# The opening of a cross-attention and feed-forward kernel: loads, second block's normalisation and values in another order

## The chip, the cores and the metric

The kernel runs on one core of a Trainium2 chip. The metric is the device time of one execution in microseconds (us), lower is better. A core has TensorE (PE, with its weight loads shown as PEld), VectorE (DVE), ScalarE (ACT), GpSimd (POOL) and SyncE (SP). SP, ScalarE and GpSimd issue DMA loads, each on a queue of its own. Every engine takes its instructions in the order in which they stand in its program.

## The reference

The input `x` has 2048 tokens of 256 features; the context has 1601 rows of 192 features. The reference normalises the tokens, adds cross-attention over the context, normalises again and adds a feed-forward layer with weights of +1 and -1. Cut to what the change touches:

```python
# 16 heads of 64; a learned null key and null value stand ahead of the 1601 context rows
x = layer_norm(layernorm(x), g_norm)
q = x @ Wq
k, v = split(context @ Wkv)
k, v = concat(null_k, k), concat(null_v, v)          # 1602 keys
sim = einsum(q, k) * scale
sim = where(mask, sim, -big)                         # the null key is always kept
out = layer_norm((softmax(sim) @ v) @ Wout, g_out)
x = x + out
x = x + ffn(layernorm(x))                            # three layers, relu between
```

## The kernel before

The work is cut into 32 units: 8 pairs of heads by 4 blocks of 512 tokens. A unit computes the scores of its block against 13 tiles of 128 keys (`exps`, L372), takes their exponential on ScalarE (L385), sums these on GpSimd (L570, L572, into `acc`), and multiplies them with the values (`weighted`, L392). The shift of each exponential is the exact maximum of the row. It is found beforehand in a cheaper number format: `max_chunk` (L335) multiplies 128 queries of both heads with 512 keys into a buffer of TensorE's accumulation memory (PSUM) and VectorE reduces it (L338). There are 12 such chunks for a block, three key chunks (`CHUNKS`) by four groups of queries, and a thirteenth (`REST`, L319 and L322) for the last 66 keys. Inside a unit the maxima of the next unit are made beside the exponentials of this one.

The first unit has no unit before it, so its keys, queries, values and maxima are made in an opening, and that is what the change is about. The order in the opening is written out by hand, under `tc.manual_schedule()`, and each engine keeps it. Its steps:

- `load_pair(0)` issues on SP the keys' and values' weights (`wa`, `wb`), with the tokens of block 0 (`load_x(0)`) between them and the query and output weights (`wq`, `wo`). The other three blocks follow on SP; the context's four chunks are issued by ScalarE; the mask (`keep`), the norm's gain (`gn_sb`), the null key and value and small things are loaded by GpSimd.
- `input_root` takes the statistics of a block on VectorE (`stats`, L75 and L76) and their root on ScalarE (L422). `input_normed` centres and scales it, on VectorE for block 0 (L87) and on ScalarE, `beside`, for the others (L141, L142). `input_turned` transposes it on TensorE (L437) into `xnT`; `project_q` makes the queries (L200), copied twice by ScalarE (L201, L202).
- `first_keys(n)` makes the keys of one chunk (L211, L212); VectorE masks them (L214) and puts the null key where a key is dropped (L215, with `drop`, the mask reversed, which GpSimd makes at L486).
- `first_values(n)` makes the values of four tiles (L259, L260), and ScalarE copies them (L262).
- `keys_stepped` turns the keys into differences on GpSimd (L248), which `exps` needs.
- `max_combined` joins the maxima (L343), `max_turned` transposes them (L348) and VectorE spreads them into `shifts` (L350).

PSUM buffers come from two pools of two: `flex` and `spare`. `slot` takes them in turn, and a buffer is free again when the engine that reads it is done.

Eight semaphores serve the loads of SP and ScalarE in turn, so a load waits on its queue until the load eight before it has landed.

In the opening before, the two key chunks, the queries and the first eight maxima come first. Then VectorE takes the statistics of block 1, and the last four chunks of maxima follow with values 0 and 1 between them, then the transposes of block 1, the rest chunk, value group 2, the queries of block 1 and value group 3:

```python
        xn = input_root(1)
        input_normed(1, *xn, beside=True)
        ...
        for t in range(4):
            max_chunk(0, 0, 3 * t + 2, slot)
            if t % 2 == 1:
                first_values(t // 2, slot)
        input_turned(1, slot)
        max_chunk(0, 0, REST, slot)
        first_values(2, slot)
        max_combined(0, 0)
        project_q(0, 1, slot)
        max_turned(0, 0)
        first_values(3, flex)
```

Of the kernel before, what the change touches and what calls it, by code (L numbers as in the profile page):

```python
# [9 lines left out]
F32 = mybir.dt.float32  # L10
F32R = mybir.dt.float32r
U8 = mybir.dt.uint8
AF = mybir.ActivationFunctionType
ALU = mybir.AluOpType
# [6 lines left out]
KEYS = M + 1  # L21
CD = 192
HEADS, DH = 16, 64
# [3 lines left out]
NB = N // 512  # L27
# [3 lines left out]
REST = 12  # L31
# [5 lines left out]
def xattn_ffn(ctx, tc, x, ctxT, mask, g_norm, null_kv, wq, wkv, wout, g_out, k0, k1, k2, s0, s1, s2, out):  # L37
# [29 lines left out]
    ones = cp.tile([128, DH], F32, name="ones")  # L67
    warm = cp.tile([128, 1], F32, name="warm")

    def stats(src, n, name):  # L70

        mv = sp.tile([128, 4, 2], F32, tag="mv", name=f"mv_{name}")
        for j in range(n):
            st = sp.tile([128, 6], F32, tag="st", name=f"st_{name}_{j}")
            nc.vector.bn_stats(st, src[:, j, :])  # L75
            nc.vector.bn_aggr(mv[:, j, :], st)  # L76
        return mv

    def rstd_of(mv, n, name, scale=1.0, bias=None):
# [64 lines left out]
    with ExitStack() as att:  # L144
# [21 lines left out]
        def load_pair(p):  # L166
            wq_t = pp.tile([128, 2, 128], F32, tag="wq", name=f"wq_{p}")
            wa_t = pp.tile([128, 2, 128], F32, tag="wa", name=f"wa_{p}")
            wb_t = pp.tile([128, 2, 128], F32, tag="wb", name=f"wb_{p}")
            wo_t = lp.tile([128, D], F32, tag="wo", name=f"wo_{p}")  # L170
            both = wkv.rearrange("r (k w) -> r k w", k=2)[:, :, ts(p, 128)]
            nc.sync.dma_start(out=wa_t, in_=both[0:128])
            nc.sync.dma_start(out=wb_t[:64], in_=both[128:CD])
            if p == 0:

                nc.gpsimd.memset(wb_t[64:], 0.0)
                load_x(0)
            else:
                nc.sync.dma_start(out=wb_t[64:], in_=both[128:CD])
            nc.sync.dma_start(out=wq_t, in_=wq[:, ts(p, 128)].rearrange("(c r) w -> r c w", c=2))  # L180
            nc.sync.dma_start(out=wo_t, in_=wout[ts(p, 128), :])
            weights[p] = (wq_t, wa_t, wb_t, wo_t)


# [65 lines left out]
        def first_values(n, get):  # L250

            v = pairs[0][1]
            tiles = range(4 * n, min(4 * n + 4, KC))
            rows = 128 if n < 3 else KLAST
            ps = get(f"psv_0_{n}")
            for i, t in enumerate(tiles):
                keys = ds(128 * t, rows)
                out_t = ps[:rows, 0, ts(i, 128)]
                nc.tensor.matmul(out_t, ctx_a[:, keys], weights[0][1][:, 1, :], start=True, stop=False)  # L259
                nc.tensor.matmul(out_t, ctx_b[:, keys], weights[0][2][:, 1, :], start=False, stop=True)  # L260
            w = len(tiles)
            nc.scalar.copy(  # L262
                v[:rows, ds(4 * n, w), :], ps[:rows, 0, : 128 * w].rearrange("p (t d) -> p t d", d=128)
            )
            if n == 0:
                nc.vector.tensor_copy(v[0:1, 0, :], nullv)

        def project_v(p, m):

# [146 lines left out]

        def input_root(b):
            mv = stats(x_sb[:, ts(b, 4), :], 4, f"x{b}")  # L420
            r = sp.tile([128, 4], F32, tag="rstd", name=f"rstd_x{b}")
            nc.scalar.activation(r, mv[:, :, 1], AF.Sqrt, bias=eps2_sb, scale=1.0 + EPS)  # L422
            return mv, r

        def input_normed(b, mv, r, beside=False):
            nc.vector.reciprocal(r, r)
            if beside:
                centred_beside(y_sb, x_sb, mv, r, b)
                return
            for j in range(4):  # L430
                centred(y_sb[:, 4 * b + j, :], x_sb[:, 4 * b + j, :], mv, r, j)
# [18 lines left out]
        def load_x(b):  # L450
            nc.sync.dma_start(out=x_sb[:, ts(b, 4), :], in_=x[ts(b, 512), :].rearrange("(c p) d -> p c d", p=128))

        load_pair(0)
        for b in range(1, NB):
            load_x(b)
        for n, (at, w) in enumerate(CHUNKS):
            skip = 1 if n == 0 else 0
            nc.scalar.dma_start(
                out=ctx_a[:, ds(at + skip, w - skip)], in_=ctxT[0:128, ds(at + skip - 1, w - skip)]
            )  # L460
            nc.scalar.dma_start(
                out=ctx_b[:64, ds(at + skip, w - skip)], in_=ctxT[128:CD, ds(at + skip - 1, w - skip)]
            )
        nc.gpsimd.memset(eps2_sb, EPS * EPS)
        nc.gpsimd.memset(eps_sb, EPS)
        make_identity(nc, ident)
        nc.gpsimd.memset(keep[:, 0:1], 0)
        nc.gpsimd.memset(ctx_a[:, 0:1], 0.0)
        nc.gpsimd.memset(ctx_b[:64, 0:1], 0.0)
        nc.gpsimd.memset(ctx_b[64:], 0.0)  # L470
        nc.gpsimd.dma_start(out=keep[:, 1:], in_=mask.partition_broadcast(128))
        nc.gpsimd.dma_start(out=gn_sb, in_=g_norm.rearrange("(c p) -> p c", p=128))
        for j in range(2):
            nc.gpsimd.dma_start(out=nullk[ts(j, DH), :], in_=null_kv[0].rearrange("(p o) -> p o", o=1))
        nc.gpsimd.memset(mcol_u8[0:1, 0:1], 1)
        nc.gpsimd.dma_start(out=mcol_u8[1:128, 0:1], in_=mask[0:127].rearrange("(p o) -> p o", o=1))
        nc.gpsimd.dma_start(
# [4 lines left out]
        )  # L482
        for j in range(2):
            nc.gpsimd.dma_start(out=nullv[:, ts(j, DH)], in_=null_kv[1:2, :])

        nc.gpsimd.tensor_scalar(drop, keep, -1.0, 1.0, ALU.mult, ALU.add)  # L486
        nc.gpsimd.dma_start(out=gout_sb, in_=g_out.partition_broadcast(128))
        for j, s in enumerate((s0, s1, s2)):
            nc.gpsimd.dma_start(out=s_sb[:, j : j + 1], in_=s.partition_broadcast(128))
        nc.gpsimd.memset(mcol, 0.0)  # L490
        nc.gpsimd.memset(maskb, 0.0)
        nc.gpsimd.memset(ones, 1.0)

        nc.scalar.activation(warm, eps_sb, AF.Sqrt)

        open_pair(0)
        xn = input_root(0)
        nc.vector.tensor_scalar(ones_r, ident, 0.0, 1.0, ALU.mult, ALU.add)
        nc.vector.tensor_tensor(pick[:, :, 0], ident[:, 0:4], ident[:, DH : DH + 4], ALU.add)
        input_normed(0, *xn)  # L500
        first_keys(0, slot)
        input_turned(0, slot)
        first_keys(1, slot)
        project_q(0, 0, slot)
        for t in range(4):
            max_chunk(0, 0, 3 * t, slot)
            if t == 1:
                first_keys(2, slot)
        for t in range(4):
            max_chunk(0, 0, 3 * t + 1, slot)  # L510
            if t == 1:
                first_keys(3, slot)
                keys_stepped(0)
        xn = input_root(1)
        input_normed(1, *xn, beside=True)

        nc.scalar.activation(warm, eps_sb, AF.Exp)

        nc.vector.tensor_scalar(maskb[:, : KC - 1], mcol_u8[:, : KC - 1], -MASKED, MASKED, ALU.mult, ALU.add)
        nc.vector.tensor_scalar(  # L520
# [1 line left out]
        )  # L522
        for t in range(4):
            max_chunk(0, 0, 3 * t + 2, slot)
            if t % 2 == 1:
                first_values(t // 2, slot)
        input_turned(1, slot)
        max_chunk(0, 0, REST, slot)
        first_values(2, slot)
        max_combined(0, 0)  # L530
        project_q(0, 1, slot)
        max_turned(0, 0)
        first_values(3, flex)
        begin.__exit__(None, None, None)
        last = None
        with tc.manual_schedule():
# [235 lines left out]
```

## Time and profile before

| what | value |
|---|---|
| median of three runs | 1332.05 us (1331.78 to 1335.83) |
| the profiled execution's own time | 1330.09 us |
| its span, first to last instruction | 1328.3 us |
| mean granted TensorE clock | 0.992 |
| TensorE busy | 1299.5 us (98%) |
| GpSimd busy | 1003.4 us (76%) |
| VectorE busy | 819.9 us (62%) |
| ScalarE busy | 618.9 us (47%) |
| TensorE busy in the first 50 us | 34.06 us |
| VectorE busy in the first 50 us | 27.86 us |
| VectorE waits for the first tokens until | 9.33 us |
| first reduction of maxima begins | 20.95 us |
| first exponential begins | 49.89 us |

The times in the profile are counted from the first instruction of the span. "L338" is line 338 of the kernel before. Busy shares over the whole span are means over the opening, 32 units and the feed-forward part; the opening has its own limits and is read from stretches of its own. A matmul in plain 32-bit numbers is listed as two instructions.

### The profile page before, as it was taken

The numbers are of one execution on the slowest core, as the hardware profiler recorded it, in microseconds if no ns is written. First come the engines' busy times: TensorE is split into PE (matmuls) and PEld (weight loads), VectorE is DVE, ScalarE is ACT, GpSimd is POOL, SyncE is SP. The second block draws the span as 40 slices with busy tenths as digits, with TensorE's granted clock in tenths as the row PEclk, the third lists the DMA queues.
The fourth block names the chain that finished last, engine by engine and source line by source line (L and its number), as shares of the span: only waits on it lengthen the run. The fifth ranks groups of instructions, "written<-read, shape, count | busy, mean of one in ns | idle before, by whom it ended". The sixth has DMA issues, their size and how long they took to land.

```text
span 1328.3 us, 16173 instructions
## 1 busy us (share of the span) xinstructions
PE 1299.5 (98%) x6528; PEld 655.3 (49%) x6528; DVE 819.9 (62%) x817; ACT 618.9 (47%) x676; POOL 1003.4 (76%) x508
## 2 busy tenths in 40 slices
PE   6989999999999999999999999999999999999998
PEld 2534444444444444444444444444444443688887
DVE  6677566666666666666666666667656784554431
ACT  1746444444454455555555555555544556421220
POOL 4478988898888988898889888888898999711100
PEclk9989999999999999999999999999999999999999
DMA  5000000000000000000000000000000010000000
GB/s 140 21 1 4 0 1 13 5 1 0 13 4 2 1 1 12 4 1 1 13 4 1 1 13 4 0 1 5 0 17 1 0 41 1 1 8 8 17 16 17
DMA packets 16091, 13.18 MB, mean 10 GB/s; under 512 B 2624, under 2 KB 15488, under 8 KB 16016
## 3 DMA queue, kind: packets, MB, share of 16 engines
q1 hardware_dynamic: 14640, 10.57, 2.8%
q10 hardware_dynamic: 896, 1.23, 0.3%
q8 instruction: 51, 0.84, 0.3%
q0 software_dynamic: 480, 0.34, 0.1%
q14 instruction: 24, 0.20, 0.0%
HBM read 10.04 MB, written 2.10 MB: 9 GB/s over the span
## 4 chain that ended last, share of the span: by engine, by line
PE 92%; DVE 4%; ACT 2%; DMA 1%; issue 1%; POOL 0%; ACTq 0%; DVEq 0%
PE sT L372 29%; PE av L392 26%; PE ps L668 10%; PE max L335 6%; PE psq L200 4%; PE po L400 4%; PE ps L691 2%; PE den L410 2%; DVE mx L338 2%; PE psv L277 2%; PE psk L225 1%; PE sT L383 1%; PE psv L289 1%; PE psk L230 1%; PE max L319 1%
## 5 line engine op out<-in xcount | busy, mean ns | idle before, releaser
L572 POOL TENSOR_TENSOR acc<-acc,e 128x1024 f32<-128x1024 f32 (+1 forms) x352 | 847.9, 2409 | 27.6
L338 DVE TENSOR_REDUCE mx<-max 128x2 f32<-128x1024 f32 x384 | 455.0, 1222 | 89.2 <-PE max L335 83.5
L385 ACT ACTIVATE e<-sT,maskb 128x1024 f32<-128x1024 f32 (+1 forms) x416 | 460.1, 1114 | 53.9 <-PE sT L383 16.8
L372 PE MATMUL sT<-qT,kT 64*128 64x512 f32 (+1 forms) x1664 | 451.1, 613 | 1.2 <-ACT e L385 1.2
L392 PE MATMUL av<-e,v 128*64 128x512 f32 (+1 forms) x1664 | 369.5, 594 | 0.2 <-ACT e L385 0.2
L335 PE MATMUL max<-kr,qr 64*128 64x512 f32 x768 | 293.3, 752 | 3.1 <-DVE mx L338 2.4
L392 PEld LDWEIGHTS av<-e,v 128*64 128x64 f32 (+1 forms) x1664 | 116.7, 137 | 237.8 <-issue 219.3
L372 PEld LDWEIGHTS sT<-qT,kT 64*128 64x128 f32 (+1 forms) x1664 | 130.2, 181 | 164.3 <-ACT e L385 155.3
L620 ACT COPY avs<-av 128x512 f32<-128x512 f32 x32 | 18.7, 586 | 323.0 <-PE av L392 323.0
L412 DVE RECIPROCAL aoT<-den 128x512 f32<-128x512 f32 x31 | 104.1, 3357 | 60.0 <-PE den L410 60.0
L570 POOL TENSOR_TENSOR acc<-e,e 128x1024 f32<-128x1024 f32 x32 | 76.8, 2399 | 80.3 <-ACT e L385 80.3
L335 PEld LDWEIGHTS max<-kr,qr 64*128 64x128 f32 x768 | 76.6, 188 | 94.0 <-DVE mx L338 46.9
L350 DVE TENSOR_TENSOR mT<-mt,pick 128x512 fp32r<-128x512 f32 x32 | 22.1, 691 | 122.1 <-PE mt L348 122.0
L668 PE MATMUL ps<-h0hi,w 128*128 128x512 f32 x256 | 79.5, 392 | 0.0
L668 PE MATMUL ps<-h0lo,w 128*128 128x512 f32 x256 | 78.9, 389 | 0.0
L120 POOL TENSOR_TENSOR y_sb<-y_sb,gout_sb 128x256 f32<-128x256 f32 x12 | 9.3, 777 | 88.8 <-DVE y_sb L87 88.8
L201 ACT ACTIVATE qr<-psq 128x512 fp32r<-128x512 f32 x32 | 19.1, 597 | 100.4 <-PE psq L200 100.4
L200 PE MATMUL psq<-xnT,wq 128*128 128x512 f32 x128 | 62.0, 608 | 2.5 <-DVE xnT L442 2.5
L657 DVE SCALAR_TENSOR_TENSOR h1lo<-ps,h1hi 128x1024 fp32r<-128x1024 f32 x16 | 19.6, 1224 | 68.3 <-ACT h1hi L656 68.2
L400 PE MATMUL po<-wo,aoT 128*128 128x256 f32 x256 | 60.5, 379 | 0.0
L656 ACT ACTIVATE h1hi<-ps 128x1024 fp32r<-128x1024 f32 x16 | 16.4, 1026 | 94.6 <-PE ps L668 94.6
L248 POOL TENSOR_TENSOR kT<-kT 128x256 f32<-128x256 f32 (+1 forms) x48 | 31.8, 661 | 35.5 <-DVE kr L237 18.8
(150 smaller groups left out, 1067.9 us busy)
## 6 DMA issues: line engine op xcount, KB each, us to landing
x_sb<-in_x SPq DMA_DIRECT2D x4, 512.0 KB, 8.6
out_x<-o SPq DMA_DIRECT2D x8, 256.0 KB, 2.1
wa<-in_wkv SPq DMA_DIRECT2D x8, 128.0 KB, 2.7
wq<-in_wq SPq DMA_DIRECT2D x8, 128.0 KB, 2.2
wo<-in_wout SPq DMA_DIRECT2D x8, 128.0 KB, 2.1
xnT<-in_k SPq DMA_DIRECT2D x1, 1024.0 KB, 5.9
wb<-in_wkv SPq DMA_DIRECT2D x15, 64.0 KB, 2.4
ctx_a<-in_ctxT ACTq DMA_DIRECT2D x2, 256.0 KB, 7.1
```

The lines of the kernel that those rows point to most:

```text
L200: nc.tensor.matmul(ps[:, 0, :], weights[p][0][:, c, :], xnT[:, b, c, :], start=c == 0, stop=c == 1)
L248: nc.gpsimd.tensor_tensor(kT[:, ds(at, w)], kT[:, ds(at, w)], kT[:, ds(at - 256, w)], ALU.subtract)
L335: nc.tensor.matmul(ps[:, j, :w], qr[rows, ts(t, 128)], kr[rows, ds(start, w)], start=True, stop=True)
L338: nc.vector.tensor_reduce(maxima[p, b][:, t, :, c], ps[:, :, :w], AX.X, ALU.max)
L372: nc.tensor.matmul(ps[:n, j, :], kT[rows, ds(128 * k, n)], qT[rows, :], start=k < 2, stop=k >= 2, skip_group_check=k >= 2,)
L385: nc.scalar.activation(e[:n], ps[:n], AF.Exp, bias=maskb[:n, k : k + 1])
L392: nc.tensor.matmul(av[ts(j, DH), 0, :], v[:n, k, ts(j, DH)], e[:n, j, :], start=k == 0, stop=k == KC - 1)
L400: nc.tensor.matmul(pv[:, t, :], aoT[:, ts(t, 128)], weights[p][3], start=True, stop=True)
L412: nc.vector.reciprocal(aoT, ps)
L570: nc.gpsimd.tensor_tensor(acc, es[0], es[1], ALU.add)
L572: nc.gpsimd.tensor_tensor(acc[:m], acc[:m], es[k][:m], ALU.add)
L668: nc.tensor.matmul(ps[:, f, :], w(c)[:, ts(2 * g + f, 128)], parts[part][:, c, :], start=i == 0, stop=i == len(steps) - 1,)
```

## The change

Nothing that is computed changes; where and when it is done does.

- The tokens of block 0 are loaded first, in two halves, one on SP and one on ScalarE's queue. ScalarE then issues only the first context chunk; chunks 1 to 3 move to SP, around the load of block 1, and the output weights and blocks 2 and 3 go behind them. The mask's load is GpSimd's first.
- The memsets of constants move from GpSimd to VectorE, ahead of the first statistics. `ones_r` and `pick` move from VectorE to GpSimd, `drop` moves from GpSimd to ScalarE, and the null value's copy from VectorE to GpSimd.
- The statistics of block 1 are taken in two halves beside the keys of chunk 1, its root stands before the query copies on ScalarE, and its normalisation on ScalarE runs beside the first maxima.
- The value groups and the transposes of block 1 stand one by one between maxima, the rest chunk comes earlier, and the queries of block 1 take their buffer from `flex`.

```diff
@@ -67,13 +67,15 @@
     ones = cp.tile([128, DH], F32, name="ones")
     warm = cp.tile([128, 1], F32, name="warm")
 
-    def stats(src, n, name):
-
-        mv = sp.tile([128, 4, 2], F32, tag="mv", name=f"mv_{name}")
+    def stats(src, n, name, mv=None):
+
+        at = 0 if mv is None else 2
+        if mv is None:
+            mv = sp.tile([128, 4, 2], F32, tag="mv", name=f"mv_{name}")
         for j in range(n):
-            st = sp.tile([128, 6], F32, tag="st", name=f"st_{name}_{j}")
+            st = sp.tile([128, 6], F32, tag="st", name=f"st_{name}_{at + j}")
             nc.vector.bn_stats(st, src[:, j, :])
-            nc.vector.bn_aggr(mv[:, j, :], st)
+            nc.vector.bn_aggr(mv[:, at + j, :], st)
         return mv
 
     def rstd_of(mv, n, name, scale=1.0, bias=None):
@@ -173,12 +175,12 @@
             nc.sync.dma_start(out=wb_t[:64], in_=both[128:CD])
             if p == 0:
 
-                nc.gpsimd.memset(wb_t[64:], 0.0)
-                load_x(0)
+                nc.vector.memset(wb_t[64:], 0.0)
             else:
                 nc.sync.dma_start(out=wb_t[64:], in_=both[128:CD])
             nc.sync.dma_start(out=wq_t, in_=wq[:, ts(p, 128)].rearrange("(c r) w -> r c w", c=2))
-            nc.sync.dma_start(out=wo_t, in_=wout[ts(p, 128), :])
+            if p > 0:
+                nc.sync.dma_start(out=wo_t, in_=wout[ts(p, 128), :])
             weights[p] = (wq_t, wa_t, wb_t, wo_t)
 
 
@@ -263,7 +265,7 @@
                 v[:rows, ds(4 * n, w), :], ps[:rows, 0, : 128 * w].rearrange("p (t d) -> p t d", d=128)
             )
             if n == 0:
-                nc.vector.tensor_copy(v[0:1, 0, :], nullv)
+                nc.gpsimd.tensor_copy(v[0:1, 0, :], nullv)
 
         def project_v(p, m):
 
@@ -416,8 +418,8 @@
 
 
 
-        def input_root(b):
-            mv = stats(x_sb[:, ts(b, 4), :], 4, f"x{b}")
+        def input_root(b, mv=None):
+            mv = mv or stats(x_sb[:, ts(b, 4), :], 4, f"x{b}")
             r = sp.tile([128, 4], F32, tag="rstd", name=f"rstd_x{b}")
             nc.scalar.activation(r, mv[:, :, 1], AF.Sqrt, bias=eps2_sb, scale=1.0 + EPS)
             return mv, r
@@ -450,28 +452,38 @@
         def load_x(b):
             nc.sync.dma_start(out=x_sb[:, ts(b, 4), :], in_=x[ts(b, 512), :].rearrange("(c p) d -> p c d", p=128))
 
+        def load_context(engine, n):
+            at, w = CHUNKS[n]
+            skip = 1 if n == 0 else 0
+            engine.dma_start(out=ctx_a[:, ds(at + skip, w - skip)], in_=ctxT[0:128, ds(at + skip - 1, w - skip)])
+            engine.dma_start(out=ctx_b[:64, ds(at + skip, w - skip)], in_=ctxT[128:CD, ds(at + skip - 1, w - skip)])
+
+
+        nc.gpsimd.memset(keep[:, 0:1], 0)
+        nc.gpsimd.dma_start(out=keep[:, 1:], in_=mask.partition_broadcast(128))
+        for half, engine in enumerate((nc.sync, nc.scalar)):
+            engine.dma_start(
+                out=x_sb[:, ds(2 * half, 2), :], in_=x[ts(half, 256), :].rearrange("(c p) d -> p c d", p=128)
+            )
+        load_context(nc.scalar, 0)
         load_pair(0)
-        for b in range(1, NB):
+        load_context(nc.sync, 1)
+        load_x(1)
+        load_context(nc.sync, 2)
+        load_context(nc.sync, 3)
+        nc.sync.dma_start(out=weights[0][3], in_=wout[ts(0, 128), :])
+        for b in range(2, NB):
             load_x(b)
-        for n, (at, w) in enumerate(CHUNKS):
-            skip = 1 if n == 0 else 0
-            nc.scalar.dma_start(
-                out=ctx_a[:, ds(at + skip, w - skip)], in_=ctxT[0:128, ds(at + skip - 1, w - skip)]
-            )
-            nc.scalar.dma_start(
-                out=ctx_b[:64, ds(at + skip, w - skip)], in_=ctxT[128:CD, ds(at + skip - 1, w - skip)]
-            )
-        nc.gpsimd.memset(eps2_sb, EPS * EPS)
-        nc.gpsimd.memset(eps_sb, EPS)
+        nc.vector.memset(eps2_sb, EPS * EPS)
+        nc.vector.memset(eps_sb, EPS)
+        nc.vector.memset(ctx_a[:, 0:1], 0.0)
+        nc.vector.memset(ctx_b[:64, 0:1], 0.0)
+        nc.vector.memset(ctx_b[64:], 0.0)
+        nc.vector.memset(ones, 1.0)
         make_identity(nc, ident)
-        nc.gpsimd.memset(keep[:, 0:1], 0)
-        nc.gpsimd.memset(ctx_a[:, 0:1], 0.0)
-        nc.gpsimd.memset(ctx_b[:64, 0:1], 0.0)
-        nc.gpsimd.memset(ctx_b[64:], 0.0)
-        nc.gpsimd.dma_start(out=keep[:, 1:], in_=mask.partition_broadcast(128))
-        nc.gpsimd.dma_start(out=gn_sb, in_=g_norm.rearrange("(c p) -> p c", p=128))
         for j in range(2):
             nc.gpsimd.dma_start(out=nullk[ts(j, DH), :], in_=null_kv[0].rearrange("(p o) -> p o", o=1))
+        nc.gpsimd.dma_start(out=gn_sb, in_=g_norm.rearrange("(c p) -> p c", p=128))
         nc.gpsimd.memset(mcol_u8[0:1, 0:1], 1)
         nc.gpsimd.dma_start(out=mcol_u8[1:128, 0:1], in_=mask[0:127].rearrange("(p o) -> p o", o=1))
         nc.gpsimd.dma_start(
@@ -482,39 +494,43 @@
         )
         for j in range(2):
             nc.gpsimd.dma_start(out=nullv[:, ts(j, DH)], in_=null_kv[1:2, :])
-
-        nc.gpsimd.tensor_scalar(drop, keep, -1.0, 1.0, ALU.mult, ALU.add)
         nc.gpsimd.dma_start(out=gout_sb, in_=g_out.partition_broadcast(128))
         for j, s in enumerate((s0, s1, s2)):
             nc.gpsimd.dma_start(out=s_sb[:, j : j + 1], in_=s.partition_broadcast(128))
         nc.gpsimd.memset(mcol, 0.0)
         nc.gpsimd.memset(maskb, 0.0)
-        nc.gpsimd.memset(ones, 1.0)
+        nc.gpsimd.tensor_scalar(ones_r, ident, 0.0, 1.0, ALU.mult, ALU.add)
+        nc.gpsimd.tensor_tensor(pick[:, :, 0], ident[:, 0:4], ident[:, DH : DH + 4], ALU.add)
 
         nc.scalar.activation(warm, eps_sb, AF.Sqrt)
 
         open_pair(0)
         xn = input_root(0)
-        nc.vector.tensor_scalar(ones_r, ident, 0.0, 1.0, ALU.mult, ALU.add)
-        nc.vector.tensor_tensor(pick[:, :, 0], ident[:, 0:4], ident[:, DH : DH + 4], ALU.add)
+
+        for keys in (ds(0, 512), ds(512, KEYS - 512)):
+            nc.scalar.activation(drop[:, keys], keep[:, keys], AF.Identity, bias=ones[:, 0:1], scale=-1.0)
         input_normed(0, *xn)
         first_keys(0, slot)
         input_turned(0, slot)
+        mv = stats(x_sb[:, 4:6, :], 2, "x1")
         first_keys(1, slot)
+        mv = stats(x_sb[:, 6:8, :], 2, "x1", mv)
+        xn = input_root(1, mv)
         project_q(0, 0, slot)
+        input_normed(1, *xn, beside=True)
+
+        nc.scalar.activation(warm, eps_sb, AF.Exp)
         for t in range(4):
             max_chunk(0, 0, 3 * t, slot)
             if t == 1:
                 first_keys(2, slot)
         for t in range(4):
             max_chunk(0, 0, 3 * t + 1, slot)
-            if t == 1:
+            if t == 0:
                 first_keys(3, slot)
                 keys_stepped(0)
-        xn = input_root(1)
-        input_normed(1, *xn, beside=True)
-
-        nc.scalar.activation(warm, eps_sb, AF.Exp)
+            else:
+                first_values(t - 1, slot) if t < 3 else input_turned(1, slot)
 
         nc.vector.tensor_scalar(maskb[:, : KC - 1], mcol_u8[:, : KC - 1], -MASKED, MASKED, ALU.mult, ALU.add)
         nc.vector.tensor_scalar(
@@ -522,15 +538,15 @@
         )
         for t in range(4):
             max_chunk(0, 0, 3 * t + 2, slot)
-            if t % 2 == 1:
-                first_values(t // 2, slot)
-        input_turned(1, slot)
-        max_chunk(0, 0, REST, slot)
-        first_values(2, slot)
+            if t == 0:
+                max_chunk(0, 0, REST, slot)
+            if t == 1:
+                first_values(2, slot)
+            if t == 2:
+                first_values(3, slot)
         max_combined(0, 0)
-        project_q(0, 1, slot)
+        project_q(0, 1, flex)
         max_turned(0, 0)
-        first_values(3, flex)
         begin.__exit__(None, None, None)
         last = None
         with tc.manual_schedule():
```

## The prediction

> **What bounds the kernel now.** I read the page first. Its chain of work that ended last gives TensorE 92% of the span, but that is a mean over 32 nearly equal units; the change touches only the stretch before the first unit. So I followed the chain of waits through the first 85 us. Columns are start, length (us), and what held the chain.
>
> ```profile
> 4.53 5.99 DMA ctx_a<-in_ctxT
> 13.74 1.97 PE xT L437 x8
> 20.95 2.36 DVE mx L338 x2
> 31.95 0.34 DVE st_x L75
> 34.74 2.34 DVE mx L338 x2
> 37.12 0.71 PE psv L259 x2
> 45.11 1.72 PE psq L200 x4
> 52.74 12.89 DVE mx L338 x11
> ```
>
> The opening is first held by loads, then mostly by VectorE (reductions, and the second block's statistics among them), then by TensorE (values, second query projection). The timeline gives its milestones (start, length, engine, line, work; in brackets the idle time before and what ended it):
>
> ```profile
> 9.33 0.43 DVE L75 BATCH_NORM_STATS2 st_x<-x_sb 128x6 f32<-128x256 f32 x1 [9.33 <-DMA x_sb<-in_x]
> 11.93 0.28 ACT L422 ACTIVATE rstd_x<-mv_x,eps_sb 128x4 f32<-128x4 f32 x1
> 20.95 2.36 DVE L338 TENSOR_REDUCE mx<-max 128x2 f32<-128x1024 f32 x2 [1.43 <-PE max L335]
> 40.59 0.22 DVE L266 COPY v<-nullv 1x128 f32<-1x128 f32 x1 [3.52 <-ACT v L262]
> 43.00 0.69 DVE L322 TENSOR_REDUCE mx<-max 128x8 f32<-128x528 f32 x1
> 49.89 1.11 ACT L385 ACTIVATE e<-sT,maskb 128x1024 f32<-128x1024 f32 x1 [1.02 <-PE sT L383]
> ```
>
> VectorE waits 9.33 us for tokens, and later 3.52 us behind a copy whose ScalarE half is itself behind the second block's normalisation. The first exponential, 49.89, ends the opening. The busy time by microsecond (columns: stretch, length, PE, PEld, DVE, ACT, POOL, granted clock, DMA share, GB/s) explains why values are slow there:
>
> ```profile
> 3.00:4.00 1.00, 0.00 (x0) 0.00 (x0) 0.00 (x0) 0.00 (x0) 1.00 (x2) 1.00 0.79 240
> 7.00:8.00 1.00, 0.93 (x1) 0.50 (x2) 0.00 (x0) 0.00 (x0) 1.00 (x2) 1.00 1.14 317
> 28.00:29.00 1.00, 0.80 (x2) 0.29 (x2) 1.00 (x2) 0.00 (x0) 0.00 (x0) 0.50 0.00 0
> 34.00:35.00 1.00, 0.75 (x5) 0.31 (x4) 0.64 (x6) 0.59 (x2) 0.12 (x1) 1.00 0.00 0
> 38.00:39.00 1.00, 1.00 (x7) 1.00 (x6) 0.00 (x0) 0.96 (x3) 0.00 (x0) 0.50 0.00 0
> ```
>
> The clock falls to 0.50 while TensorE only feeds reductions, and the values behind them run at half rate (a pair of 128x128 steps 0.43 us there, 0.22 us at 43.8).
>
> After the first exponential everything follows everything else: no load or constant is late there, so a shorter opening should move the rest by as much. I therefore split the 49.89 us in four and rebuild each: tokens landed 9.33; to the first reduction 11.62; from there to the last reduction of the first block (43.69) 22.74; from there to the exponential 6.20.
>
> **Tokens first: 9.33 to 4.7.** Today the 512 KB are third on SP, issued at 2.12, 7.2 us to landing. After, two halves are issued at 0.74 on SP and ScalarE's queue; only the mask broadcast (200 KB, POOL) competes. The first context chunk (255.5 KB) took 2.9 us; by the slices 0.54 MB had moved by 4.0, and about 0.66 MB must: some 4.3, plus 0.4 for completion. Bounds: 3.6 (as that chunk) to 7.9 (0.74 + 7.2). I take 4.7, nearer the chunk, as both have nothing ahead of them. The Trainium skill (Trainium Kernel Development and Optimization, Key Constraints) says that all issuing queues share the same 16 DMA engines; on that, two queues alone win only issue time and 3.6 is out of reach. The DMA share near 1 with two queues from 5 us on agrees.
>
> **To the first reduction: 11.62 to 13.25.** Statistics 4 x 0.535 = 2.14, to 6.85. Root to start of centring took 0.53, as here; ScalarE is no longer stuck until 10.53 behind its own eight context loads (three remain), so it waits for nothing: 7.45. Centring 2.19. The first keys stand before the transposes on TensorE; their weights and context now lie behind the tokens. Together 0.58 MB more at 290 GB/s: start about 6.4, two steps of 1.7 at half clock and gaps, to 10.0. Transposes 1.2 (between 1.09 and 1.97): 11.2. Then ScalarE's and VectorE's halves of the evacuation 0.69 + 0.75: 12.75 with gaps. New on this path: two tiles of second-block statistics 1.07; keys of chunk 1 (0.69 + 0.75); two more tiles 1.07: 16.4. The second root (0.30) stands before the query copy (0.60) on ScalarE: 17.35. First maxima 0.54: 17.95. Queries are ready sooner, so the 2.14 of statistics cost nearly all of themselves here and are bought back below.
>
> **The reductions: 22.74 to 18.55.** VectorE has 12 reductions x 1.175 = 14.1, keys 1.4 and 0.45, mask bias 0.2, rest 0.69: 16.9. The statistics and their wait (31.86 to 34.72, 2.86) are gone, so is the 3.52 wait. With values spread, I step through with two score buffers of each pool: at full clock a value group is 1.75 us against 1.175 for a reduction, and TensorE is late once or twice: 0.85. If the clock falls before the first group, that takes 3.4 us and the sum of holes is 2.45. I take the middle, 1.65.
>
> **The tail: 6.20 to 2.9.** Today a value group and the query projection stand before the transpose of the maxima (46.83), and the last value group behind it. After, only half a score step (0.86) and the projection (1.72) follow the last maxima on TensorE, mostly beside the last reduction. Transpose at 1.0 after it, then 0.69 for the shifts and two short steps: 2.9.
>
> Sum: 4.7 + 13.25 + 18.55 + 2.9 = 39.4, against 49.89: 10.5 us earlier.
>
> **Costed at nothing.** VectorE's memsets: on POOL 0.31 + 1.43 + some 0.6, so done by 3.1; idle until 4.7 covers them. The drop mask on ScalarE: by its rows of 0.60 (512 columns) and 1.11 (1024) about 1.7, between the root (7.25) and the evacuation (11.2); it costs only if the mask lands after 9.5, and at today's 7.9 us from an issue at 0.85 it lands at 8.75. nullk and gn, behind fewer POOL instructions, are issued near 2.1 and 3.2 instead of 4.77 and 4.02; with today's 7.1 and 7.6 they land at 9.2 to 9.8 and 10.8, needed at 10.8 and 11.2: little slack, up to 0.5 if slower. Later POOL issues wait for earlier landings, and behind them stand ones_r and pick (VectorE 0.35; on POOL between 0.2 and 0.8 each), needed near 36. The null value's copy follows key stepping (4.35) and is due only at the first weighted sum. On SP the second block's load waits for the first half's landing: issue near 5.3; by bytes ahead it lands near 11, by today's 9.3 us at 14.6, needed at 12.75: 0 to 1.9 us, behind which chunk-1 keys are queued. Output weights, blocks 2 and 3 and the next pair's weights move behind it, all needed after 70 us. The second normalisation's 8 ScalarE steps (4 us) and table load run beside reductions; no value copy waits before 26.
>
> **The clock.** The trace drops at 27 and recovers at 33.6 and 40.2 after about 3 us of unbroken work. TensorE: Matmul & The Clock Gate (the Trainium skill, Part 1) puts this down to a free-running 3.4 us window; by it the phase is chance, and my 0.85 or 2.45 (1.6 us of result) would be drawn per execution. The spacing of the trace's changes, 27, 33.6, 37.4, 40.2, agrees roughly.
>
> **Time.** The profiled execution took 1330.09 (span 1328.3): 1319.6. The shown runs' median lies 1.96 above it; on that scale 1321.6.
>
> **Rivals.**
> (1) Loads do not speed up by order: latency under load rules. Tokens land at 7.9 (+3.2), the second block is issued at 8.5 and lands at 17.8, against 15.95 needed (+1.9). Gain 5.4: 1326.7. For it: small POOL loads also take 6 to 8 us. Against: the first loads took 2.9 to 3.8.
> (2) More than forecast: clock stays full, tokens at 3.6, second root hidden: 10.5 + 0.8 + 1.1 + 0.6 = 13: 1319.0.
> (3) Slower: values among the maxima make TensorE the bound because the clock stays at 0.50. From 17.4: 12 x 0.8 maxima, keys 3.4 + 0.8, values 10.2 + 1.2, transposes 2.0, rest 1.2 = 28.4, to 45.8; score half and projection 5.1, then 2.5: 53.4, or 3.5 later: 1335.6. It needs the half clock over three quarters of the stretch. Against: two recoveries within 3 us of full work.
> (4) It does not do what it says downstream: unit 0 ends behind something fixed, such as POOL's accumulation. Against: that chain starts with the second exponential (52.40). Time 1332.
>
> **How the numbers follow.** Forecast 0.60, (1) 0.20, (2) 0.10, (3) 0.05, (4) 0.05. A measurement tells about 0.3%, 4.0 us, from no change. Faster by that: forecast, (2) and most of (1): 0.87; within: (4) and a little of (1): 0.08; slower 0.05. The range takes in (1) and the clock's and landings' bounds, leaves out (3), (4) and the far end of (2): 1318.0 to 1327.5.
>
> **What would show it.** In the changed profile: first statistics near 4.7; first L340 reduction near 18; no statistics among reductions; VectorE holes under 2.5 us in all; first exponential near 39.4; the later chain as before. Statistics at 8 mean (1); a clock row of 0.50 from 18 to 36 means (3); an early exponential without a shorter span means (4).

## The result, and the profile after

The changed kernel takes 1325.49 us (median of four runs, 1323.26 to 1326.04) against 1331.94 for the kernel before (four runs): a ratio of 0.9948 with an interval of 0.9932 to 0.9963. It is faster by 6.45 us, where 10.5 were forecast. Its profiled execution took 1326.04 (span 1324.2), the longest of its four, against 1330.09 for the profiled one before, so the two traces differ by 4.05 only; in them the first exponential moved by 4.51. The sum of the forecast was built on the traced execution, and there it brought 4.05 of 10.5.

The chain of waits after, for the first 60 us (start, length, what held the chain):

```profile
1.23 7.00 DMA wa<-in_wkv
...
8.37 2.05 PE psk L213 x2
...
18.62 0.03 ACT rstd_x L424
...
19.45 0.85 PE max L337 x4
20.31 2.00 PE psk L213 x2
...
27.58 0.80 PE psv L261 x2
...
48.24 12.91 DVE mx L340 x11
```

The tokens are gone from the chain; the key weights (`wa`) now hold its beginning. The second block's root stands in it, and TensorE (keys, values, maxima) holds the stretch in which VectorE should have been the bound. After the opening comes the same long row of reductions as before, 12.91 where it was 12.89. The milestones, from the timeline (start, length, engine, line, work; in brackets the idle time before it and what ended that):

```profile
4.35 0.43 DVE L77 BATCH_NORM_STATS2 st_x<-x_sb 128x6 f32<-128x256 f32 x1 [1.11 <-DMA x_sb<-in_x]
18.62 0.30 ACT L424 ACTIVATE rstd_x<-mv_x,eps_sb 128x4 f32<-128x4 f32 x1 [4.36 <-DVE mv_x L78]
19.45 0.85 PE L337 MATMUL max<-kr,qr 64*128 64x512 f32 x4 [2.48 <-ACT qr L203]
20.00 2.36 DVE L340 TENSOR_REDUCE mx<-max 128x2 f32<-128x1024 f32 x2 [0.81 <-PE max L337]
23.78 0.69 DVE L216 TENSOR_TENSOR kT<-psk,keep 128x512 f32<-128x512 f32 x1 [1.43 <-PE psk L214]
32.13 1.23 DVE L340 TENSOR_REDUCE mx<-max 128x2 f32<-128x1024 f32 x1 [1.89 <-PE max L337]
35.26 1.23 DVE L340 TENSOR_REDUCE mx<-max 128x2 f32<-128x1024 f32 x1 [1.91 <-PE max L337]
40.13 2.36 DVE L340 TENSOR_REDUCE mx<-max 128x2 f32<-128x1024 f32 x2 [0.43 <-PE max L337]
45.38 1.11 ACT L387 ACTIVATE e<-sT,maskb 128x1024 f32<-128x1024 f32 x1 [0.38 <-PE sT L385]
```

Read with the prediction's four terms: tokens at 4.35, first reduction 15.65 later at 20.00, the reductions 22.5 long (to 42.5), the tail 2.89. Between the reductions VectorE has four holes (idle stretches), 1.43 + 1.89 + 1.91 + 0.43 = 5.66 us; all wait for TensorE. The busy time by stretches shows why (stretch, length, PE, PEld, DVE, ACT, POOL, granted clock, DMA share, GB/s):

```profile
4.00:5.00 1.00, 0.00 (x0) 0.00 (x0) 0.61 (x3) 0.00 (x0) 1.00 (x3) 1.00 1.32 339
5.00:6.00 1.00, 0.00 (x0) 0.00 (x0) 0.93 (x5) 0.00 (x0) 1.00 (x2) 1.00 0.69 123
6.00:7.00 1.00, 0.00 (x0) 0.00 (x0) 0.60 (x4) 0.30 (x1) 1.00 (x3) 1.00 0.87 220
7.00:8.00 1.00, 0.00 (x0) 0.00 (x0) 0.96 (x4) 0.38 (x1) 0.39 (x2) 1.00 1.20 199
8.00:9.00 1.00, 0.63 (x1) 0.50 (x2) 0.54 (x2) 1.00 (x2) 0.31 (x1) 1.00 1.11 154
...
20.00:23.00 3.00, 3.00 (x6) 1.17 (x4) 2.35 (x2) 2.90 (x7) 0.00 (x0) 0.50 0.77 148
...
30.00:34.00 4.00, 4.00 (x20) 3.34 (x20) 1.47 (x2) 0.59 (x1) 3.46 (x6) 0.55 0.00 0
```

Two things were not in the forecast. From 5 to 9 us the queues move 123 to 220 GB/s, not 290, and the key weights issued at 1.23 are there only at 8.24. And the clock is at 0.50 from 19.9 to 23.3 and again from 26.8 to 33.6, right when VectorE waits for keys and values.

### The profile page after: what moved, and what is told of

Read it like the earlier page. It is cut to its first block, busy times and chain, and to the rows that moved or that the text cites. A ratio compares the mean times of both kernels' runs of the same rounds, so it can differ in the third digit from the quotient of the medians.

```text
span 1324.2 us, 16178 instructions
## 1 busy us (share of the span) xinstructions
PE 1298.3 (98%) x6528; PEld 654.0 (49%) x6528; DVE 816.9 (62%) x821; ACT 620.6 (47%) x678; POOL 1001.3 (76%) x503
## 4 chain that ended last, share of the span: by engine, by line
PE 93%; DVE 3%; ACT 2%; issue 1%; DMA 1%; POOL 0%; SPq 0%; ACTq 0%; DVEq 0%
PE sT L374 29%; PE av L394 26%; PE ps L684 10%; PE max L337 7%; PE psq L202 4%; PE po L402 4%; PE ps L707 2%; PE den L412 2%; PE psv L279 2%; PE psk L227 1%; PE sT L385 1%; DVE mx L340 1%; PE psv L291 1%; PE psk L232 1%; PE max L321 1%
## 5 line engine op out<-in xcount | busy, mean ns | idle before, releaser
L636 ACT COPY avs<-av 128x512 f32<-128x512 f32 x32 | 18.7, 586 | 323.0 <-PE av L394 323.0
L250 POOL TENSOR_TENSOR kT<-kT 128x256 f32<-128x256 f32 (+1 forms) x48 | 31.8, 662 | 37.0 <-DVE kr L239 18.7
```

Of the source, the lines that this page charges most:

```text
L250: nc.gpsimd.tensor_tensor(kT[:, ds(at, w)], kT[:, ds(at, w)], kT[:, ds(at - 256, w)], ALU.subtract)
```

## The experiments

Every kernel was also profiled once; "first reduction", "reductions" (their length) and "first exponential" are from that execution, times and ratios from all runs, each ratio against the kernel before as it ran alongside. Diffs are against the changed kernel. For comparison, it has 20.00, 22.5 and 45.38. The traces carry scatter of their own: in the eight with the loads and the opening order of the changed kernel, the first keys begin anywhere from 7.82 to 8.72. So half a microsecond at the first reduction tells nothing.

**The two halves of the change alone.** `order_only` takes loads and constants back and keeps the new order; `loads_only` keeps loads and constants and takes back the order:

```diff
 # order_only: load_pair(0) issues block 0 between wb and wq again, context on ScalarE's queue,
 #             memsets and drop on GpSimd, ones_r and pick on VectorE;
 #             order of the opening as changed (null value's copy on GpSimd)
 # loads_only:
-        mv = stats(x_sb[:, 4:6, :], 2, "x1")
         first_keys(1, slot)
-        mv = stats(x_sb[:, 6:8, :], 2, "x1", mv)
-        xn = input_root(1, mv)
         project_q(0, 0, slot)
...
+        xn = input_root(1)
+        input_normed(1, *xn, beside=True)
...
+            if t % 2 == 1:
+                first_values(t // 2, slot)
```

> Loads and constants as before, order of the compute steps as changed (with the null value's copy on GpSimd). Theory A (half clock): the holes among the reductions belong to the order, so first to last reduction takes about 22 us again, the tail 2.9, first reduction near 22.5 (tokens at 9.3, two more microseconds of statistics ahead): first exponential near 48, 2 us earlier than before, time about 1330. Rival B (late weights starve TensorE): with the weights at 4.5 again the reductions take about 18.5: first exponential near 44, time about 1326.

> Loads and constants as changed, order of the compute steps as before. Both theories: transposes end near 13.5 as in the changed kernel, no statistics ahead of the first reduction, so that begins near 18.8; then 22.7 to the last reduction and 6.2 to the exponential as before: 47.7, 2.2 us earlier than before, time about 1330. If the loads gain more than 3 us alone, the order costs time.

`order_only`: 1326.45 (1325.58 to 1327.11), ratio 0.9961 [0.9948, 0.9973]; first reduction 23.40, reductions 19.8, first exponential 45.99. `loads_only`: 1325.79, 0.9957 [0.9939, 0.9975]; 18.39, 21.6, 45.96, with a tail of 6.0. Each half alone brings 3.9 us at the first exponential; together they bring 4.5. Against `order_only` the changed kernel begins its reductions 3.4 us sooner and takes 2.7 us longer over them: what the loads win is lost again before the last reduction. In `order_only` the clock stays at 1.00 until 29.3, and the reductions are nearer to rival B's 18.5 than to theory A's 22. `loads_only` won 3.9 us at the first exponential where 2.2 were expected: by the medians (1325.79 and 1325.49) the new order adds nothing measurable to the new loads.

**Is it the clock?** `filled_gaps` adds six matmuls whose products nobody reads, in the places where TensorE idles; the work is only more, so a gain would speak for the clock:

```diff
         project_q(0, 0, slot)
+        filler("fill_a", 3)          # three 128x128x512 steps into a buffer of the pools
...
+            if t == 3: filler("fill_b", 1)
+                filler("fill_c", 1)  # after the last keys
+                if t == 1: filler("fill_d", 1)
```

> The changed kernel with six more matmuls whose results nobody reads, in TensorE's gaps: three of 0.85 us after the first queries, one each after the fourth maxima chunk, after the last keys and after the sixth maxima chunk. Theory A (the half clock makes the holes): granted clock stays at 1.00 from 20 to 34, holes of VectorE fall from 5.7 to under 2.5, first exponential near 42, time 3 us under the changed kernel. Rival C (the holes come from whole value groups between single reductions, whatever the clock): no change or up to 2 us more.

1323.78 (1323.36 to 1324.54), 0.9941 [0.9922, 0.996]; 20.83, 20.6, 44.27. The same stretches as above:

```profile
20.00:23.00 3.00, 3.00 (x11) 1.11 (x12) 2.17 (x2) 2.90 (x7) 0.00 (x0) 1.00 0.70 123
...
30.00:34.00 4.00, 4.00 (x32) 3.33 (x30) 1.23 (x1) 0.85 (x2) 2.85 (x5) 1.00 0.02 4
```

With more work the clock stays at 1.00 all through the opening and the stretch from 30 to 34 holds 32 matmuls instead of 20. The reductions are 1.9 us shorter although they begin 0.83 later. So the half clock is worth some 2 us, 1.7 between the medians. But holes of 2.04, 1.19 and 0.44 remain, where under 2.5 in all were expected (a filler of mine stands in the first). The timeline has the second (this kernel's lines are shifted by six):

```profile
34.17 1.23 DVE L346 TENSOR_REDUCE mx<-max 128x2 f32<-128x1024 f32 x1 [1.19 <-PE max L343]
```

Behind a value group VectorE waits 1.19 at full clock too.

**The added wait on ScalarE.** The second root stands ahead of the query copies on ScalarE, and it waits for all four tiles of statistics. `root_behind_queries` puts it behind:

```diff
         mv = stats(x_sb[:, 6:8, :], 2, "x1", mv)
-        xn = input_root(1, mv)
         project_q(0, 0, slot)
+        xn = input_root(1, mv)
```

> The changed kernel with one wait taken away: the second block's root stands behind the two query copies on ScalarE instead of ahead of them. If that wait makes the TensorE gap (16.97 to 19.45) which lets the clock fall: query copy at 17.0, first maxima at 17.6, keys of chunk 2 by 20, clock at 1.00 until 24 at least, VectorE's hole of 1.43 before the keys of chunk 2 gone, first exponential near 43.5, time about 1.5 us under the changed kernel. If VectorE's own statistics set the first reduction and the clock does not matter: first exponential 45 to 45.4.

1323.25 (1322.38 to 1323.97), 0.9945 [0.993, 0.9959]; 18.56, 20.6, 41.99. Timeline:

```profile
16.50 0.60 ACT L203 ACTIVATE qr<-psq 128x512 fp32r<-128x512 f32 x1 [2.75 <-PE psq L202]
17.15 0.74 PE L337 MATMUL max<-kr,qr 64*128 64x512 f32 x4 [0.69 <-ACT qr L203]
```

The query copy starts at 16.50 instead of 18.82, TensorE's gap before the first maxima is 0.69 instead of 2.48, and the clock is still 1.00 at 20. The hole before the keys of chunk 2 (1.43) is gone. The root now starts at 18.09. The wait was the larger part of what is missing: 3.4 of some 6 us at the first exponential, of which 0.55 was there before the root already (the first keys start at 7.82, not 8.37), and 2.2 between the medians. The clock still falls to 0.50 once, from 22.9 to 29.7, among the first values.

**Values ahead of the maxima.** Two of the value groups that stand among the reductions are put where TensorE would idle:

```diff
         project_q(0, 0, slot)
+        first_values(0, slot)
...
             if t == 2:
                 first_keys(2, slot)
+                first_values(1, slot)
...
-            else:
-                first_values(t - 1, slot) if t < 3 else input_turned(1, slot)
+            elif t == 3:
+                input_turned(1, slot)
```

> The changed kernel with value group 0 moved into TensorE's 2.5 us gap before the first maxima and value group 1 behind the keys of chunk 2, real work in place of idle time. Theory A: clock stays up, two groups (3.4 us each at half clock) are gone from among the later reductions: first exponential near 41.5, time about 4 us under the changed kernel. Rival C (whole groups between reductions) says the same for the reductions between 27 and 35 but keeps the clock low: about 2.5 us under it.

1319.80 (1319.55 to 1321.63), 0.9913 [0.9894, 0.9933]; 19.70, 19.37, 41.18. This is the best kernel of the study by its median, 11.4 us under the kernel before; its longest run (1321.63) is under the shortest of the changed kernel (1323.26). The stretches (columns as above):

```profile
28.00:32.00 4.00, 2.79 (x23) 1.86 (x22) 4.00 (x7) 1.27 (x2) 3.51 (x6) 1.00 0.02 6
32.00:36.00 4.00, 4.00 (x20) 3.34 (x21) 2.74 (x4) 0.59 (x1) 0.45 (x1) 0.57 0.00 0
```

And from its timeline, the first maxima:

```profile
19.16 0.73 PE L337 MATMUL max<-kr,qr 64*128 64x512 f32 x4 [1.09 <-ACT qr L203]
```

One value group fills most of the wait for the second root (a gap of 1.09 is left of 2.48), and from 28 to 32 VectorE is busy 4.00 of 4.00. The clock falls later, at 32.6, when two value groups are left, one of them of 66 rows.

**Both, and statistics moved.** Three more kernels:

```diff
 # values_early_root = values_early, and input_root(1, mv) behind project_q(0, 0)
 # stats_later = the changed kernel with the statistics of block 1 behind maxima t = 0 and t = 2,
 #               root behind t = 2, normalisation behind t = 3
 # values_early_stats = values_early and stats_later together
```

> Early values (group 0 behind the first queries, group 1 behind the keys of chunk 2) and the root behind the query copies. The values already fill the gap, so the root's wait should be worth little here: first exponential 40.5 to 41.2, time within 1 us of the variant with early values alone (1319.8).

> The changed kernel with the second block's statistics and its root moved back from ahead of the first reduction to among the first four (first half behind the first reduction, second half behind the third), so the query copies no longer wait for that root. If the statistics ahead of the first reduction open the TensorE gap (16.97 to 19.45) that lets the clock fall: first reduction near 18, clock at 1.00 until 25 or later, first exponential near 43, about 2.5 us under the changed kernel. If the holes are due to whole value groups alone, the 2.1 us of statistics come back among the reductions and the first exponential stays within 1 us of 45.4.

> Early values and the second block's statistics among the first reductions, with the order of transposes and keys as in the changed kernel. First reduction near 18.3 as with late statistics, 19.0 of VectorE work from there, holes 1.5 to 2.5, tail 2.1: first exponential near 41, time near 1319.5. If it is over 1322 like the combination, the statistics among the reductions are what cost there, and not the transposes' place.

`values_early_root`: 1320.49 (1318.81 to 1322.59), 0.9924 [0.9911, 0.9937]; 18.92, 21.1, 42.11: within a microsecond of `values_early`, as expected: the two remedies fill the same gap. `stats_later`: 1322.74, 0.9934 [0.9919, 0.9949]; 18.23, 22.3, 43.37: about as `root_behind_queries`. Of the 2.0 us at the first exponential 1.8 are won at the first reduction; the 2.1 us of statistics that now stand among the reductions are paid for by smaller holes (3.28 instead of 5.66). `values_early_stats`: 1323.83 (1323.11 to 1324.2), 0.9947 [0.9934, 0.996]; 18.18, 22.2, 43.31: 4.0 us worse than `values_early` and over the 1322 at which the statistics among the reductions were to be blamed, not near the 1319.5 that was hoped for. The clock is at 0.50 from 28.3 to 38.6. Statistics are cheaper ahead of the reductions, where the change put them, once TensorE has work beside them.

**The start.** Keys stand ahead of the transposes on TensorE, and their weights land late. `transposes_first` swaps them. `combined` does so too; it has the queries ahead of the second key chunk, the statistics as in `stats_later`, and value groups 0 and 1 behind the first and the fourth maxima. The swap:

```diff
-        first_keys(0, slot)
         input_turned(0, slot)
+        first_keys(0, slot)
```

> The changed kernel with the transposes of block 0 ahead of the first keys on TensorE. Theory: the weights that land at 8.2 to 9.6 behind the tokens hold the transposes up, which could start at 8.4 and end near 10.4 (13.5 in the changed kernel); the keys then end near 13.5, evacuation of the transposes lies beside them, and the first reduction comes 1 to 1.5 us earlier, near 18.7. Rival: VectorE's chain from the keys on sets the time and nothing moves (19.5 to 20).

> Transposes ahead of the keys, queries ahead of the second key chunk, statistics among the reductions, value group 0 behind the first maxima and group 1 behind the fourth. VectorE's work from the first keys on is 1.6 + 0.75 for block 0, 1.45 for the second keys, 16.9 for reductions and the rest and 2.1 for statistics. Keys at 13.5, first reduction near 17, last near 37.5 with 1.5 us of holes, tail 2.1 to 2.9: first exponential near 40, about 1 us under the variant with early values alone, time near 1319. If TensorE's gaps or the clock return, it stays at 41 to 42.

`transposes_first`: 1325.89, 0.9956 [0.9941, 0.9971]; 20.09, 21.7, 45.05. No gain, where the first reduction was expected at 18.7. The timeline tells why:

```profile
7.77 1.94 PE L439 MATMUL xT<-ident,y_sb 128*128 128x128 f32 x8 [7.77 <-DVE y_sb L89]
11.71 0.69 ACT L440 ACTIVATE xnT<-xT,gn_sb 128x512 f32<-128x512 f32 x1 [2.15 <-DMA gn_sb<-in_g_norm]
```

The transposes are done 3.8 us sooner, but their evacuation needs the gain, 1 KB, which is issued at 3.7 and lands 8.0 us later. In the changed kernel the slow keys hide that. `combined`: 1322.42, 0.993 [0.9914, 0.9947]; 17.18, 20.9, 41.33. It has the earliest reductions of all and not the best time (1319 was expected); the half clock, from 27.5 to 34.3, and statistics among the reductions take it back.

**Are early tokens worth anything?** `weights_first` issues `load_context(nc.scalar, 0)` and `load_pair(0)` ahead of the two token halves; `weights_first_old_order` does the same in `loads_only`:

```diff
+        load_context(nc.scalar, 0)
+        load_pair(0)
         for half, engine in enumerate((nc.sync, nc.scalar)):
...
-        load_context(nc.scalar, 0)
-        load_pair(0)
```

> The changed kernel with the key and query weights and the first context chunk issued ahead of the token halves. Theory (tokens early are of no use while TensorE waits for weights): weights land near 4.5, tokens near 7.5, the first keys run from 4.6 to 9.2, transposes end near 13.5 as in the changed kernel; first exponential within 1 us of 45.4. Rival (tokens first is what gains): first reduction 2 us or more later than 20.0, time 2 us over the changed kernel.

> Order of the compute steps as before, loads and constants as changed, but the weights and the first context chunk ahead of the token halves. Theory (tokens early bring nothing while TensorE waits for weights; the gain of the loads is the mask, the constants and the shorter ScalarE queue): tokens at 9.0, transposes end near 14.3, first reduction 18.9 to 19.4, first exponential 46 to 47, time within 1 us of the loads alone (1325.8). Rival (the gain is tokens first): first reduction near 20.9, first exponential near 49, time near 1330.

`weights_first`: 1324.37 (1324.13 to 1325.28), 0.9947 [0.9932, 0.9962]; tokens 8.98, first reduction 21.53, reductions 19.8, first exponential 44.17. With the tokens 4.6 us later, the time is no worse. Keys run at 4.21 while the tokens come, and the granted clock does not fall before 27.5:

```profile
20.98 0.73 PE L337 MATMUL max<-kr,qr 64*128 64x512 f32 x4 [1.75 <-ACT qr L203]
```

`weights_first_old_order`: 1329.11 (1327.84 to 1329.76, 11 runs), 0.998 [0.997, 0.999]; tokens 9.06, first reduction 20.72, first exponential 47.64. So in the old order early tokens are worth 3.3 us (1329.11 against 1325.79, ratios 0.998 and 0.9957) and the rest of the new loads and constants about 2. My theory that early tokens bring nothing fell for the old order and held for the new one. There the sooner start goes with a half clock from 19.9 on and the later one does not; that this is the reason is argued from one trace each.

## Why the prediction was right, and where it was off

The sign, the mechanism and the range were right: the opening is shorter, its gain comes out at the end, 1325.49 lies between 1318.0 and 1327.5. The size was 0.61 of the forecast between the medians and 0.39 between the traces (4.05 of 10.5), for which the sum was made. Two terms carry that: together they were 6.35 us too short.

- **Tokens, 4.7.** Measured 4.35 for the first half (the second landed at 4.74, ahead of its statistics). By 4.30 the queues had moved 0.67 MB, as counted. Rival (1), latency that order can't change, is false for the tokens, and half true for what stood behind them.
- **To the first reduction, 13.25: mis-sized by 2.4.** The step that failed is "0.58 MB more at 290 GB/s: start about 6.4". From 4.30 to 8.24 the mean rate was 199 GB/s, at which 0.58 MB are there at 7.2; the other microsecond is 0.2 MB of loads that I had not counted and that moved in the same time. The keys began at 8.37 and the transposes ended at 13.54, not 11.2. Centring took 1.38 instead of 2.19 and was done at 8.54, beside the first keys. From there on, 6.46 us to the first reduction were forecast as 6.75. The Trainium skill (Trainium Kernel Development and Optimization, Key Constraints) says that all issuing queues share the same DMA engines; the DMA share of 1.32, 1.20 and 1.11 in three of the five rows after 4 us agrees, and what the tokens won the weights paid: 4.21 for the first keys in `weights_first`, 8.37 here.
- **The reductions, 18.55: mis-sized by 3.95.** The work was 16.84 (forecast 16.9); the holes were 5.66, not 1.65. "Late once or twice: 0.85" was too little even at full clock: in `order_only`, `filled_gaps`, `stats_later` and `weights_first` a hole of 1.19 remains behind a value group at clock 1.00, as the group and the next maxima together are longer than one reduction. My own half-clock end, 2.45, was passed too: the clock fell already at 20 and a second time at 27. The second fall has its like without that wait (27.0 in the kernel before, 22.9 in `root_behind_queries`, 23.8 in `stats_later`); what set off the first is the second root "before the query copy (0.60) on ScalarE". I charged it 0.30 on the path to the first reduction; on TensorE's it makes a gap of 2.48, against 0.69 without it. Without it the clock at 20 was 1.00 and the first exponential 3.4 us earlier (`root_behind_queries`). That a filled gap keeps the clock is shown (`filled_gaps`). Before the first maxima, gaps of 0.69, 1.09 and 1.75 did not make it fall, 2.48 and 3.60 (`transposes_first`) did; the last section tells what else it hangs on.
- **The tail, 2.9.** Measured 2.89.
- **Costed at nothing.** The memsets ended at 3.24, ahead of the tokens. The drop mask, 7.62 to 9.44, lay ahead of the evacuation at 13.57. The gain landed at 11.7, in time only because the keys were late. The second block landed just before its statistics (issue 5.25, 9.7 us, first tile at 14.97). On GpSimd `ones_r` took 0.67 and `pick` 0.19, inside the bounds.
- **The clock as chance.** The rule that I weighed would have drawn 0.85 or 2.45 by phase. I read the changes of the clock before as 27, 33.6, 37.4 and 40.2; in tenths they are at 27.0, 33.8, 37.2 and 40.65, and that fits a window better than "roughly" (last section). The clock did differ between executions: the changed kernel's four had means of 0.992 to 0.995 over the span, and the time went with it (1326.04 and 1326.03 at 0.992, 1323.26 at 0.995). But the 2.4 us between 4.05 and 6.45 are scatter of both kernels: the profiled execution before lies 1.85 under its median, the one after 0.55 over its own. That the median came nearer to the forecast than the trace is luck. In the profiled execution the half clock takes 10.2 us in the opening and 10.2 more from 74.5 to 84.8, so it is not known where the execution at 0.995 saved it.
- **Rivals (2) to (4).** (2) needed the full clock and did not come. (3) had the right mechanism, a half clock among values, over 10.2 us (19.9 to 23.3 and 26.8 to 33.6) of the 22.5, not three quarters; so the sign held. (4) is false: of 4.51 us at the first exponential, 4.05 are there at the end of the trace.

## What to carry to other kernels

A gain in a prologue is worth what the clock leaves of it: before pulling work forward, follow TensorE through the new order and look for gaps ahead of the stretch that it will bound, and move independent matmuls into them (here two value groups, 5.7 us between medians). A wait put on one engine's queue must be priced for every engine behind it: the root cost ScalarE 0.30 and TensorE 1.8 (a gap of 2.48 against 0.69). Two halves that each bring 3.9 us alone need not add: price them against the same next bound.

## What the runs showed of the hardware that was not expected

- **The clock changes on a grid of 3.41 us.** Read in tenths of a microsecond, the granted clock of the changed kernel falls at 19.92, rises at 23.33, falls at 26.75 and rises at 33.57. Cut at these points and at their multiples, its windows are (columns as above):

```profile
16.51:19.92 3.41, 0.93 (x6) 0.30 (x4) 2.21 (x8) 1.30 (x4) 0.00 (x0) 1.00 1.11 319
19.92:23.33 3.41, 3.41 (x8) 1.17 (x4) 2.36 (x2) 3.28 (x8) 0.00 (x0) 0.50 0.70 138
23.33:26.75 3.42, 2.20 (x13) 1.20 (x12) 2.94 (x4) 1.79 (x3) 0.00 (x0) 1.00 0.00 0
26.75:30.16 3.41, 2.84 (x14) 2.58 (x13) 3.38 (x5) 0.00 (x0) 0.89 (x2) 0.50 0.00 0
30.16:33.57 3.41, 3.41 (x15) 2.75 (x15) 1.31 (x2) 0.59 (x1) 3.10 (x6) 0.50 0.00 0
```

  In all fourteen traces, over the first 100 us, every stretch of half clock lasts 3.41, 6.82 or 10.24, one, two or three windows. The grid lies elsewhere in each: counted back to the start of the span, at 2.85 here, at 3.10 in the kernel before, at 0.93 in `transposes_first`. The gap of 2.48 lies whole in one window and leaves it 0.93 of work; what it would do if the grid split it between two, no run here shows. From 16 to 100 us, in the thirteen traces whose opening shows the grid, each of the 24 windows at full clock with TensorE busy for less than 0.56 of it was followed by half clock, and none with more than 0.65 was; of the ten between, four were. Of the windows at half clock, the 37 with TensorE busy for less than 0.89 kept it, and 27 of the 28 from 0.90 on freed it. The exception is in `values_early_stats`:

```profile
31.74:35.16 3.42, 3.42 (x22) 2.94 (x19) 2.97 (x3) 1.26 (x3) 0.70 (x1) 0.50 0.02 5
35.16:38.57 3.41, 3.41 (x16) 2.42 (x15) 0.96 (x1) 0.59 (x1) 0.00 (x0) 0.50 0.00 0
```

  The first of these is as full as the second and did not free it; no run here tells why. TensorE: Matmul & The Clock Gate, Part 1, of the Trainium skill has a free-running window of about 3.4 us and the clock freed after a busy one; all these rows but one agree. So my "recoveries within 3 us of full work" depended on where the work began: the changed kernel worked without a break from 27.58 and was freed at 33.57, because the window from 26.75 on was only 2.84 full. Busy time of a matmul is modelled, so the shares are those of the profile.
- **Matmuls can run at half rate beside a clock column of 1.00.** Ahead of the first change that a trace records, the column reads 1.00. The first key step of the changed kernel takes 2.05 at 8.37, and the like step of the second chunk 1.02 at 13.37. In `weights_first` that second one still takes 1.92, at 14.07. The price of an early step is read from its row, not from the clock.
- **A VectorE step that meets the drop mask on GpSimd is held.** Before, centring took 2.19 beside it (11.98 to 13.53 on GpSimd) and in the changed kernel, with the mask on ScalarE, 1.38. In `order_only`, where it is on GpSimd again (11.85 to 13.40), `ones_r` on VectorE took 2.06, from 11.58, instead of 0.19, and centring began 1.25 us later than before. This is most of why its reductions began at 23.40 and not at the 22.5 that was expected; in the changed kernel the 0.81 that centring gained stood behind the weights and brought nothing.
- **A small load in a crowd is slow.** The gain's 1 KB took 8.0 us to land in the changed kernel, 1.0 us longer than 128 KB of key weights that were issued 2.5 us before it.
